# A top-p attention step with two more slots before its key transposes, and features plus bias formed one layer earlier

## The chip, the cores and the metric

The kernel runs on one core of one Trainium2 chip. Five engines work side by side, each through its own instructions in order: TensorE (PE, with its weight loads shown as PEld), VectorE (DVE), ScalarE (ACT), GpSimd (POOL) and SyncE (SP). SP, ACT and POOL also issue DMAs. The metric is the device time of one execution in microseconds (us); lower is better.

## The reference, cut to what matters

Four graph layers work on 4096 nodes with 256 features, each with the residual and a layer norm. Layer 0 is a product with the dense-stored, mostly sparse adjacency. Layer 1 runs two steps of a top-p attention beside two steps of a random walk:

```python
x = _layernorm(x + A @ (x * W))                       # layer 0
# layer 1, for n in range(2):
A  = _top_p_attention(Xa, W1, W2, W3)                 # softmax, keep the top 90 %
Xf = R @ Xf                                           # R = (S + I) / row sums
Xa = A @ Xa
Z  = Z + Xf @ U1[n].T + Xa @ U2[n].T
# after both steps:
h = X + Z
x = _layernorm(X + layernorm(h) * ln_g + ln_b)        # X: what layer 0 left
```

Layers 2 (attention over neighbours) and 3 (sum over neighbours, then a product with weights) follow. What matters here is that the end of layer 1 needs the sum X + ln_b once for each block of 128 nodes.

## The kernel before, in words

The nodes form 32 blocks of 128 (NT = 32). There are five stages in a row.

*Layer 0* (about 0 to 536 us). The first 16 blocks are dense (`dense_0`): panels of the adjacency come by SP and are multiplied on PE. While that goes on, `find_columns` looks for the nonzero columns of the other blocks and `list_columns` makes lists of them. The last 16 blocks are listed (`listed_0`): POOL gathers blocks of the adjacency (`pc`, in `pack`) and rows of features (`xg`, in `listed_steps`) by those lists. Each block has an end, `out_0`, in two halves. The first half (L475 to L481) is a layer norm on DVE and gives the features xi. The second half (L483 to L493) transposes them, projects them to keys kT and queries, writes the table `tab` (features and values for keys), and multiplies with U1 (po, L464), which gives qs and qp; ACT issues the stores. `later` (L497) starts the first half at once and runs the second half when two more ends have come. In this stage the framework's planner orders the instructions by estimated times, with program order as priority.

*Step one of layer 1* (536 to 1245 us) is written out by hand. A loop of slots (L1207) advances every active generator `narrow(I)` by one stage in each slot, the oldest first, and starts a new one every 8 slots (SLOTS), so that five or six are active. One slot of the random walk's stream `r_stream` follows (one gather each, its multiplication five slots later), and in odd slots one round of `lists`, which makes the lists of the first 16 blocks. On PE, ACT, DVE and POOL the instructions stand in exactly this order.

The stages of `narrow(I)` by slot number, counted from its start:

| slots | what is done | engine |
|---|---|---|
| 0 to 8 | logits in four chunks (multiplications 0 to 3, L1014), their exponentials (L1029), largest values (L1020) | PE, ACT, DVE |
| 9, 10 | sort of the largest (L736, L738), target (tgt, L1035), then uv and the threshold mid (L1050) | DVE, POOL |
| 11 to 20 | marks (L1058), counts (cs), ranks, offsets (pd, off, step, since), positions (pi, L1089), indices idx (L1098) | ACT, PE, DVE |
| 21 to 23 | five gathers of rows g from `tab` (L1102) | POOL |
| 24 | empty | |
| 25, 26 | key transposes pk (L1110), copy kg | PE, ACT |
| 27 to 30 | logits of the listed columns sl, reload of the features x0, exponential w, mask and its sum (L1123) | PE, SP, ACT, DVE |
| 31 to 35 | transposes pw, copy wT, weighted sum psa (L1137), new features xa, transposes ptx | PE, ACT |
| 36 to 41 | copy xT, product po (L464), copy v (L884) and features plus bias xb (L886, stored to `xbd`), z (L890), scaling and store of z, projection psq | ACT, PE, POOL, DVE, SP |

The slots of one narrow that are equal modulo 8 meet those of the others, so a cycle of 8 slots holds each stage once. The logits and the wide transposes share two banks (tag lg), the gathered rows have two sets of five tiles.

*Step two* (1245 to 2390 us) is a second top-p attention; its `out_1` (L919) loads xb back. *Layers 2 and 3* end the kernel at 2819 us. The code below is that which the change touches.

Of the kernel before, what the change touches and what calls it, by code (L numbers as in the profile page):

```python
# [11 lines left out]
F32 = mybir.dt.float32  # L12
# [6 lines left out]
P = 128  # L19
N = 4096  # L20
D = 256
# [48 lines left out]
def gnn_kernel(ctx: ExitStack, tc: tile.TileContext, x, pair, W0, W1, W2T, W3T, U1T, U2T,  # L70
               ln_g, ln_b, Hv, W3L, b3, out):
    nc = tc.nc
# [7 lines left out]
    scopes, pools = [], {}  # L80
# [28 lines left out]
    def row_bcast(v, n, name, tag=None):  # L109
        t = const.tile([P, n], F32, name=name, tag=tag or name)  # L110
        nc.gpsimd.dma_start(t, bass.AP(tensor=v.tensor, offset=v.offset, ap=[[0, P], [1, n]]))
        return t
# [4 lines left out]
    def rows(I):  # L117
        return slice(I * P, (I + 1) * P)


    XW = []
    w0b = row_bcast(W0, D, "w0b")
    for j in range(NT):
        t = big.tile([P, D + 1], F32, name=f"xw_{j}", tag=f"xa{j}", padded_shape=[P, D + 2])
        nc.scalar.dma_start(t[:, :D], x[rows(j), :])
# [14 lines left out]
    w1 = work.tile([DA, D], F32, name="w1", tag="y")  # L140
# [89 lines left out]
    def transposed(tiles, name, apart=False):  # L230

        n = 2 * len(tiles)
        pt = bank([P, 4, P], "ptx", "ms")
        for s, t in enumerate(tiles):
            for h in range(2):
                nc.tensor.transpose(pt[:, 2 * s + h, :], t[:, h * P:(h + 1) * P], ident)  # L236
        xT = work.tile([P, 4, P], F32, name=name, tag="xT")
        def turn():
            nc.scalar.copy(xT[:, :n, :], pt[:, :n, :])  # L239
        if apart:  # L240
            return turn, xT
        turn()
        return xT
# [23 lines left out]
    def layernorm(o, y, own=True):  # L267
        m, rs = norm_stats(y, own)
        nc.vector.tensor_scalar(o, y, m, rs, op0=OP.subtract, op1=OP.mult)
# [8 lines left out]
    def project(xT, n, I, more=None):  # L278

        half, b = divmod(I, NT // 2)  # L280
        r, other = (slice(h * DA, (h + 1) * DA) for h in (half, 1 - half))
        c = rows(n * (NT // 2) + b)
        ps = bank([P, 2, P], "psq", "ms")
        for h in range(2):
            nc.tensor.matmul(ps[:, 0, :], wqk[:, h, r.start:r.start + P], xT[:, h, :], start=(h == 0), stop=(h == 1))
        if more is not None:
            for h in range(2):
                nc.tensor.matmul(ps[:, 1, :DA], xT[:, h, :], wqk[:, h, :DA], start=(h == 0), stop=(h == 1))
        yield
        nc.scalar.copy(kT[r, c], ps[r, 0, :])  # L290
        q = work.tile([P, P], F32, name="q")
        nc.scalar.copy(q[other, :], ps[other, 0, :])
        (nc.sync if n else nc.scalar).dma_start(qd[n][I], q[other, :])
        if more is not None:
            nc.scalar.copy(more[:, D:], ps[:, 1, :DA])

    def run(gen):
        for _ in gen:
            pass
# [144 lines left out]
    qpd, zd, xbd = ([dram.tile([P, D], F32, name=f"{k}_{I}", tag=f"{k}{I}") for I in range(NT)] for k in ("qp", "z", "xb"))  # L444
# [7 lines left out]
    def load_u(w, pool):  # L452

        u = pools[pool].tile([P, 2, 2 * D], F32, name="u", bufs=1)
        for n in range(2):
            nc.gpsimd.dma_start(u[:, :, n * D:(n + 1) * D], w[n].rearrange("(c p) o -> p c o", p=P))
        return u
# [3 lines left out]
    def times_both(xT, u):  # L461
        po = bank([P, 2, D], "po", "ms")
        for h in range(2):
            nc.tensor.matmul(po.rearrange("p a b -> p (a b)"), xT[:, h, :], u[:, h, :], start=(h == 0), stop=(h == 1))  # L464
        return po
# [8 lines left out]
    def out_0(I, ps, sums, xin):  # L474
        nc.vector.tensor_scalar_add(rone[:, I:I + 1], sums, 1.0)  # L475
        nc.vector.reciprocal(rinv[:, I:I + 1], rone[:, I:I + 1])
        y = work.tile([P, D], F32, name="y")
        nc.vector.tensor_mul(y, ps[:, :D], w0b)
        nc.vector.tensor_add(y, y, xin)
        xi = pools["w0"].tile([P, TW], F32, name="xi", bufs=4)  # L480
        layernorm(xi[:, :D], y)  # L481
        yield
        xT = transposed([xi], "xT0")  # L483
        for _ in project(xT, 0, I, xi):
            pass
        nc.scalar.dma_start(tab[rows(I), :], xi)
        po = times_both(xT, U[0])
        qs = pools["w0"].tile([P, D], F32, name="qs")
        nc.scalar.copy(qs, po[:, 1, :])
        nc.scalar.dma_start(qtab[rows(I), :], qs)  # L490
        qp = pools["w0"].tile([P, D], F32, name="qp")
        nc.vector.scalar_tensor_tensor(qp, po[:, 0, :], rone[:, I:I + 1], qs, op0=OP.mult, op1=OP.add)
        nc.scalar.dma_start(qpd[I], qp)  # L493

    waiting = []

# [7 lines left out]
    def listed_0(I):  # L504
        pse = bank([P, 2, LC], "pse", "lg")[:, 0, :]
        ps = acc_tile("R")
        es = es_tile()
        parts = list(pack(I, es[:, 0, :], es[:, 1, :]))
        listed_matmul(ps, x, D, I, parts)
        for k in range(2):  # L510
            nc.tensor.matmul(pse[:, k:k + 1], es[:, k, :], ones, start=True, stop=True)
        nc.scalar.copy(edge[:, I:I + 1], pse[:, 0:1])
        for m, (a, b) in enumerate(pieces(I)):
            nc.scalar.dma_start(packed[I][m], parts[m][:, :b - a])
        later(out_0(I, ps, pse[:, 1:2], XW[I][:, :D]))

    def dense_0(I):
        ps = acc_tile("A")
        blocks = list(range(I * NEW, min((I + 1) * NEW, NT)))
        adj_matmul(ps, XW, I, seen, D + 1, lambda c: [find_columns(J) for J in blocks[c:c + 1]])  # L520
        later(out_0(I, ps, ps[:, D:D + 1], XW[I][:, :D]))

    late = LE
    for I in range(LE):
# [4 lines left out]
        if I >= LE // 2:  # L529
            n = (11 * (I - LE // 2 + 1)) // (LE // 2) - (late - LE)  # L530
# [13 lines left out]
    banks(lg=2)  # L544
    enter(e=2, gat=8, sp=2, w1=2)
    U[1] = load_u(U2T, "w1")
    gb, bb, hvb = row_bcast(ln_g, D, "gb"), row_bcast(ln_b, D, "bb"), row_bcast(Hv, D, "hvb")
    facts = [{k: const.tile([P, NT], F32, name=f"f{n}_{k}") for k in "sfuhxrd"} for n in range(2)]
    n_listed = const.tile([P, NT], F32, name="n_listed")
    both_sums = const.tile([P, NT, 2], F32, name="both_sums")  # L550
# [298 lines left out]
    def reload(src, I, name="xin", pool=None):  # L849
        t = (pools[pool] if pool else work).tile([P, D], F32, name=name, bufs=2)  # L850
        nc.sync.dma_start(t, src[rows(I), :D])
        return t
# [18 lines left out]
    def z_tile():  # L871
        return work.tile([P, D], F32, name="z")
# [4 lines left out]
    def out_a0(I, xa, x0, v):  # L877
        turned, xT = transposed([xa], "xT1", True)
        yield
        turned()  # L880
        yield
        po = times_both(xT, U[1])
        yield
        nc.scalar.copy(v, po[:, 1, :])  # L884
        xb = pools["w1"].tile([P, D], F32, name="xb")
        nc.gpsimd.tensor_add(xb, x0, bb)  # L886
        nc.sync.dma_start(xbd[I], xb)
        yield
        z = z_tile()
        nc.vector.tensor_add(z, po[:, 0, :], x0)  # L890
        yield
        nc.scalar.activation(z, z, AF.Copy, scale=rone[:, I:I + 1])
        nc.sync.dma_start(zd[I], z)
        yield from project(xT, 1, I)
# [101 lines left out]
    def narrow(I):  # L996
# [104 lines left out]
        for k in range(NB):  # L1101
            gather(g[k], tab, idx, slice(k, k + 1))  # L1102
            if k % 2:
                yield
        yield
        yield
        kg = sp.tile([DA, NB * P], F32, name="kg", bufs=1)
        pk = wide("pk")
        for k in range(NB):
# [7 lines left out]
        x0 = reload(tab, I, "x0r", "w1")  # L1117
# [22 lines left out]
        yield  # L1140
        V.append(v_tile(I))
        yield from out_a0(I, xa, x0, V[I])

    def wide(name):
# [45 lines left out]
    def r_stream():  # L1190
        due, t = [], 0
        for b in list(range(LE, NT)) + list(range(LE)):
            if b == 0:
                run(lists)
            for _ in r_one(b, lambda f: due.append((t + LATE, f))):
                t += 1
                while due and due[0][0] <= t:
                    due.pop(0)[1]()
                yield
        for _, f in due:  # L1200
            f()

    everything = {getattr(mybir.EngineType, k) for k in ("PE", "Activation", "DVE", "Pool")}
    with tc.manual_schedule(engines=everything):
        active, side, credit, n = [], r_stream(), 0.0, 0
        started = 0
        while active or started < NT:  # L1207
            if n % SLOTS == 0 and started < NT:
                active.append(narrow(started))
                started += 1  # L1210
            for g in list(active):
                if next(g, active) is active:
                    active.remove(g)
            credit += PACE
            while credit >= 1.0:
                next(side, None)
                credit -= 1.0
            if n % 2:
                next(lists, None)
            n += 1  # L1220
        run(side)
# [221 lines left out]
    def with_all_columns():  # L1443
        U[0], U[1] = load_u(U1T, "w0"), load_u(U2T, "w1")
        for I in range(LE, NT):
            ps = acc_tile("A")
            adj_matmul(ps, rows4(x, 1), I, width=D + 1)
            xin = reload(x, I)
            run(out_0(I, ps, ps[:, D:D + 1], xin))
# [82 lines left out]
```

## Time and profile before

| what | value |
|---|---|
| median of 3 runs | 2817.93 us (2816.73 to 2818.35) |
| the profiled execution | 2821.13 us, of which its span 2819.3 us |
| granted TensorE clock, mean | 0.908 of full speed |
| busy share of the span | PE 80%, DVE 75%, POOL 63%, PEld 56%, ACT 54% |
| DMA | 354.25 MB, mean 126 GB/s |
| gathers on POOL in step one | 160 of g, 969 ns each; 180 of xg from qtab, 979 ns each |
| xb on POOL (L886) | 32, 736 ns each, first at 623.4 us, last at 1234.3 us |
| transposes of keys (L1110) | 160, 282 ns each, first at 586.7 us, last at 1218.0 us |

The busy time of an engine says how much it has to do, and not whether the end waits for it. The waits say which instruction stood idle and what ended the idleness; the chain of waits follows the last instruction back in time. Where several engines take turns in a loop, the one that ends each wait last sets the pace.

### The profile page before, as it was taken

How to read it: one execution, taken by the hardware profiler on the slowest of the kernel's cores; microseconds unless marked ns; L12 is line 12 of the kernel's file. 1: busy time of each engine (PE TensorE's matmuls, PEld its weight loads, DVE VectorE, ACT ScalarE, POOL GpSimd, SP SyncE). 2: the span in 40 equal slices, each digit the busy share in tenths (PEclk: the TensorE clock that was granted, in tenths of full speed). 3: DMA queues.
4: the chain of work that ended last, by engine and by line, in shares of the span. 5: the costliest groups of instructions: out<-in, count | busy, mean ns of one | idle time of the engine just before them, and what ended most of it. 6: DMA issues, size and time to landing. Idle time of an engine off the chain costs nothing.

```text
span 2819.3 us, 38065 instructions
## 1 busy us (share of the span) xinstructions
PE 2256.6 (80%) x10712; PEld 1589.9 (56%) x10712; DVE 2109.3 (75%) x6442; ACT 1520.5 (54%) x2432; POOL 1781.4 (63%) x2840
## 2 busy tenths in 40 slices
PE   6778789778988888853788888888888887597997
PEld 4556576444444444531566666666656666476785
DVE  4777566688777778715688999999999997477574
ACT  0001111255566566537688888888888983464111
POOL 1002644355677667753788888888888874675774
PEclk9989898888898989875899999999999998799998
DMA  9995765444445445540212111111111112686664
GB/s 269 266 269 169 195 193 168 133 135 145 126 136 146 140 137 156 147 128 2 83 50 63 52 52 44 45 52 49 61 44 40 42 35 77 210 245 193 194 208 126
DMA packets 354060, 354.25 MB, mean 126 GB/s; under 512 B 35120, under 2 KB 307008, under 8 KB 353840
## 3 DMA queue, kind: packets, MB, share of 16 engines
q1 hardware_dynamic: 272224, 183.10, 22.3%
q0 software_dynamic: 51008, 144.85, 18.0%
q10 hardware_dynamic: 30608, 23.77, 2.6%
q8 instruction: 88, 1.44, 0.2%
q14 instruction: 132, 1.08, 0.1%
HBM read 298.69 MB, written 52.89 MB: 125 GB/s over the span
## 4 chain that ended last, share of the span: by engine, by line
PE 33%; DVE 27%; DMA 12%; POOL 11%; ACT 10%; issue 7%; ACTq 0%; DVEq 0%; POOLq 0%; SPq 0%
DMA half<-in_pair 5%; PE acc L204 4%; DVE cand L759 4%; PE po L464 4%; PE psa L228 3%; PE acc L433 3%; DVE tmp L753 3%; PE lg L1014 3%; PE acc L1363 3%; POOL xg L379 3%; DVE top L736 2%; DVE rest L738 2%; PE acc L1160 2%; DMA g<-tab,idx 2%; ACT junk L676 2%
## 5 line engine op out<-in xcount | busy, mean ns | idle before, releaser
L228 PE MATMUL psa<-v,eT 128*128 128x256 f32 x2048 | 510.7, 397 | 90.3 <-ACT eT L219 90.2
L228 PEld LDWEIGHTS psa<-v,eT 128*128 128x128 f32 x2048 | 398.2, 198 | 171.2 <-ACT eT L219 116.4
L204 PE MATMUL acc<-xw,panel 128*128 128x257 f32 x1024 | 265.5, 416 | 64.3 <-DMA panel<-in_pair 53.4
L379 POOL DMA_INDIRECT xg<-in_x,idx_x x72 | 71.5, 993 | 326.8 <-DVE idx_a L356 243.7
L204 PEld LDWEIGHTS acc<-xw,panel 128*128 128x128 f32 x1024 | 207.9, 208 | 117.8 <-issue 41.8
L676 ACT ACTIVATE junk<-e,h 128x4096 bf16<-128x4096 f32 x64 | 237.4, 3709 | 37.2 <-POOL h L656 32.0
L678 ACT ACTIVATE junk<-e,h 128x4096 bf16<-128x4096 f32 x64 | 238.3, 3723 | 0.1
L217 PE MATMUL pt<-ident,e 128*128 128x128 f32 x1024 | 157.8, 285 | 85.1 <-DVE e L805 57.9
L379 POOL DMA_INDIRECT xg<-ttab,idx_x x180 | 177.3, 985 | 67.1 <-issue 34.2
L379 POOL DMA_INDIRECT g<-tab,idx x160 | 155.0, 969 | 94.2 <-issue 50.9
L569 PE MATMUL lg<-kT,qi 64*128 64x512 f32 x512 | 157.7, 694 | 69.9 <-ACT junk L640 66.8
L379 POOL DMA_INDIRECT xg<-qtab,idx_x x180 | 176.2, 979 | 55.7 <-issue 45.6
L379 POOL DMA_INDIRECT pc<-in_pair,idx_a x180 | 174.3, 968 | 52.1 <-issue 45.8
L759 DVE MAX8 cand<-tmp 128x8 f32<-128x128 f32 x1024 | 203.3, 276 | 1.2
L217 PEld LDWEIGHTS pt<-ident,e 128*128 128x128 f32 x1024 | 130.3, 147 | 130.0 <-issue 90.7
L1020 DVE MAX8 cand<-e 128x8 f32<-128x256 f32 x512 | 179.1, 412 | 28.5 <-ACT e L1029 22.1
L1014 PE MATMUL lg<-kT,qi 64*128 64x512 f32 x512 | 168.7, 740 | 33.4 <-ACT e L1029 28.1
L219 ACT COPY eT<-pt 128x512 f32<-128x512 f32 x256 | 145.0, 592 | 85.6 <-PE pt L217 85.5
L239 ACT COPY xT<-ptx 128x256 f32<-128x256 f32 (+1 forms) x96 | 42.4, 441 | 266.2 <-PE ptx L236 129.9
L379 POOL DMA_INDIRECT xg<-x3d,idx_x x146 | 139.8, 957 | 67.2 <-issue 40.3
L637 ACT ACTIVATE e<-lg 128x1024 f32<-128x1024 f32 x128 | 131.6, 1028 | 67.6 <-PE lg L569 63.7
L1029 ACT ACTIVATE e<-lg 128x1024 f32<-128x1024 f32 x128 | 130.7, 1021 | 57.6 <-PE lg L1014 57.1
(323 smaller groups left out, 5645.8 us busy)
## 6 DMA issues: line engine op xcount, KB each, us to landing
panel<-in_pair SPq DMA_DIRECT2D x200, 256.0 KB
half<-in_pair SPq DMA_DIRECT2D x64, 512.0 KB
pc<-pk SPq DMA_DIRECT2D x55, 320.0 KB
pc<-pk SPq DMA_DIRECT2D x45, 256.0 KB
tab<-xi ACTq DMA_DIRECT2D x33, 160.0 KB
pc<-pk SPq DMA_DIRECT2D x23, 192.0 KB
x2d<-x SPq DMA_DIRECT2D x32, 129.0 KB
x<-x2d SPq DMA_DIRECT2D x32, 129.0 KB
```

The source lines that it names most:

```text
L204: nc.tensor.matmul(ps[:, :width], a[:, k, :], r, start=(j == 0), stop=stop and j == NT - 1)
L217: nc.tensor.transpose(pt[:, k, :], e[:, (g * 4 + k) * P:][:, :P], ident)
L219: nc.scalar.copy(eT[g], pt)
L228: nc.tensor.matmul(ps[:, :D], eT[g][:, k, :], rhs[j][:, :D], start=(j == 0), stop=stop and j == NT - 1)
L379: nc.gpsimd.indirect_dma_start(out=o, out_offset=None, in_=src, in_offset=bass.IndirectOffsetOnAxis(ap=idx[:, c], axis=0))
L569: nc.tensor.matmul(ps[:, h, :], qi[r, :], kT[r, (n * NC + c) * LC:][:, :LC], start=True, stop=True)
L637: nc.scalar.activation(both(e, c), ps, AF.Exp, accum_out=s8[:, c:c + 1])
L676: nc.scalar.activation(junk_tile(), e, AF.Relu, bias=h, scale=-1.0, accum_out=part)
L678: nc.scalar.activation(junk_tile(), e, AF.Sign, bias=h, scale=-1.0, accum_out=below)
L759: nc.vector.max(cand[:, c * (NS // 2) + g, :], w[:, g * SEG:(g + 1) * SEG])
L1014: nc.tensor.matmul(lgs[c][:, k, :], qi[r, :], kT[r, c * LC:(c + 1) * LC], start=True, stop=True)
L1020: nc.vector.max(cand[:, b, :], e[:, b * SEG0:(b + 1) * SEG0])
```

## The change

Four edits. The row of ln_b (bb) is loaded to all partitions at the start of the program and not at the start of layer 1. The second half of `out_0` adds it to the features on POOL and stores the sum (`xbd`) by ACT; `out_a0` in step one no longer does so (there SP stored it). Behind the gathers, `narrow` yields four times where it yielded twice, so that every stage from the key transposes on stands two slots later, in slots 27 to 43. The rounds of `lists` begin in slot 3 and not in slot 1.

```diff
-    w0b = row_bcast(W0, D, "w0b")
+    w0b, bb = row_bcast(W0, D, "w0b"), row_bcast(ln_b, D, "bb")
@@ out_0
         nc.scalar.dma_start(qpd[I], qp)
+        xb = pools["w0"].tile([P, D], F32, name="xb")
+        nc.gpsimd.tensor_add(xb, xi[:, :D], bb)
+        nc.scalar.dma_start(xbd[I], xb)
@@ start of layer 1
-    gb, bb, hvb = row_bcast(ln_g, D, "gb"), row_bcast(ln_b, D, "bb"), row_bcast(Hv, D, "hvb")
+    gb, hvb = row_bcast(ln_g, D, "gb"), row_bcast(Hv, D, "hvb")
@@ out_a0
         nc.scalar.copy(v, po[:, 1, :])
-        xb = pools["w1"].tile([P, D], F32, name="xb")
-        nc.gpsimd.tensor_add(xb, x0, bb)
-        nc.sync.dma_start(xbd[I], xb)
         yield
@@ narrow
             if k % 2:
                 yield
-        yield
-        yield
+        for _ in range(4):
+            yield
         kg = sp.tile([DA, NB * P], F32, name="kg", bufs=1)
@@ the loop of slots
-            if n % 2:
+            if n % 2 and n > 2:
                 next(lists, None)
```

## The prediction

> **What bounds the kernel now.** I read the page first: the chain that ended last is spread over PE 33%, DVE 27%, DMA 12% and POOL 11%, so no engine bounds the whole, and the change must be judged in its two stages. Next came the busy times by stage (columns: stretch, its length, busy PE, PEld, DVE, ACT, POOL, then PEclk, DMA share, GB/s): the part of layer 0 in which listed tiles run, and step one.
>
> ```profile
> 259.00:536.00 277.00, 224.56 (x992) 170.21 (x991) 164.77 (x491) 35.34 (x136) 141.40 (x146) 0.89 0.60 172
> 536.00:1245.00 709.00, 591.94 (x3307) 335.20 (x3307) 529.46 (x1851) 404.24 (x720) 479.76 (x593) 0.89 0.50 143
> ```
>
> In step one PE is busy for 83% and POOL for 68%, but two gathers start 1.25 us apart though each is busy 0.95, so POOL is nearly full too. Then the waits of 560 to 1240 us (total us, times, longest):
>
> ```profile
> PE pk L1110 <- DMA g<-tab,idx: 54.5, 36, 4.4
> ...
> PEld lg L1014 <- ACT e L1029: 34.4, 21, 3.3
> ...
> ACT marks L1058 <- DVE mid L1050: 31.0, 24, 3.5
> ...
> DVE z L890 <- ACT v L884: 21.3, 13, 7.0
> ...
> DVE uv L1045 <- POOL tgt L1035: 13.0, 11, 3.0
> ```
>
> PE waits 54.5 us for gathered keys, but it also waits for exponentials, which come late because ACT waits for the threshold (mid) from DVE. The chain of waits shows both in one cycle of eight slots:
>
> ```profile
> 909.95 2.00 ACT marks L1058
> 911.95 1.01 ACT e L1029 x2
> 912.96 0.04 issue
> 913.00 1.13 PE lg L1014 x4
> ...
> 922.48 4.25 DMA g<-tab,idx
> 926.73 0.04 issue
> 926.77 0.30 PE pk L1110
> ```
>
> So there are two loops of about equal length. Loop A: indices (DVE) end at 913.59, five gathers leave POOL until 923.42, the last key transpose starts at 926.77, and the next indices follow it on PE and DVE. Loop B: logits multiplication 3, its exponential, the largest values, the sort, mid, marks, exponential 1, multiplication 2, and on to multiplication 3. By the timeline, multiplication 2 of narrow 8 starts at 714.56 and that of narrow 31 at 1169.17: 23 cycles of 19.77 us. Eight cycles in which loop B alone rules (it starts 0.14 us after exponential 1 at both ends) take 18.37, 20.68, 19.87, 18.72, 18.71, 19.78, 18.14, 19.55: 19.23 on average. Removing the wait for the gathers is therefore not worth 54.5 us.
>
> Last, the POOL rows around an addition of features and bias, and a stretch of layer 0's chain:
>
> ```profile
> 917.82 0.73 POOL L886 TENSOR_TENSOR xb<-x0r,bb 128x256 f32<-128x256 f32 x1
> ...
> 918.71 0.97 POOL L379 DMA_INDIRECT g<-tab,idx  x1 [0.16 <-issue]
> ```
> ```profile
> 415.27 5.03 DMA pc<-in_pair,idx_a
> 420.43 0.69 DVE pr L400
> ```
>
> One addition holds POOL for 0.89 us, in the midst of the five gathers. In layer 0, POOL's gathers of pair blocks and their landing are themselves on the chain.
>
> **What the Trainium skill says.** "TensorE: Matmul & The Clock Gate", Part 1: an idle window of about 3.4 us halves PE's clock. The trace agrees: in 987.4 to 1001.0, right after waits for gathers, PEclk is 0.50; po (four passes) takes 3.31 us at 895.56 against 1.72 elsewhere. Same page, "Architectural detail": ACT, DVE and GpSimd are strict FIFO. Here the store of a packed block held ACT until 420.48 and the copy xT behind it until 421.82. "Trainium Kernel Development and Optimization", Key Constraints: transfers issued from SP, ACT and POOL share the same 16 DMA engines, so the store's move from SP to ACT moves no bytes elsewhere; only its time changes (no row before tests it). "GPSIMD Engine Reference", Engine selection: a two-input elementwise operation there is about twice as slow as on VectorE; the trace has 736 ns (L886) against 414 ns (L890, same shape).
>
> **The change, part by part.** Sums are made against the profiled execution: 2821.13 us (span 2819.3), 3.2 us above the median of 2817.93.
>
> *Two slots, gain on the gathers.* Between the slot of the last gather and that of the transposes lie four slots (some 10 us) where two lay. New loop A: indices, 0.76 us to the first gather, seven gathers of 1.25 less a gap (8.45), 3 us to land, then pk and pi (0.8) and the next indices (2.1): 15 us, below loop B, so this wait should nearly vanish. Its worth is how much later than exponential 1 multiplication 2 now starts, beyond 0.14: in narrows 9, 10, 12 to 15, 19 to 22 and 29 it is 0.58, 4.02, 0.08, 1.63, 1.23, 0.90, 0.16, 1.97, 1.89, 2.02 and 1.89, in sum 16.4 us. The averages above give (19.77 − 19.23) × 23 = 12.4. I take 16.4, bounds 12 and 30 (halved clock behind a wait lengthens the multiplications after it).
>
> *Two slots, cost on the order.* Everything from the transposes to the projection shifts by two places in the cycle. (1) z (L890, 0.41 us, 0.45 with its gap) stood in DVE's order before the largest values of chunk 3, in the shadow of ACT's exponential; now it stands between them and the sort, inside loop B: 0.45 × 28 cycles = +12.6. It also waits for v and so for po, now one slot after multiplication 3: at full clock po ends as DVE comes free, so +0; at half clock up to 1.7 us more. Bounds 0 (PE later anyway) and +25. (2) The mask and its reciprocal (L1123, L1125: 1.1 us) leave a gap of DVE for the place just before chunk 3; where multiplication 3 starts under 4.5 us after multiplication 2 (six of 23 cycles) this costs about 0.6: +3.6. (3) PE's work between the same multiplications is equal (po 1.72 leaves, ptx 0.43 and sl 1.3 come in). Logits banks still alternate; multiplication 3 now needs exponential 2's bank, free 3.9 us after multiplication 2 against a measured minimum of 3.75: nothing. Gather tiles g have two sets; the weighted sum that frees them moves to two slots ahead of the gathers that reuse them: no wait. The tail's two empty slots cost nothing, as the last narrow waits for its gathers there anyway.
>
> *Addition off step one.* POOL loses 32 × 0.89 = 28 us, SP 32 stores (and the 171 us that SP spent waiting for POOL). POOL's target (tgt) stands behind the gathers and held DVE's uv for 13.0 us, inside loop B; without 0.89 us ahead of it and with z in front of uv that goes: −13.0, bounds 0 and −13. The last narrow's gathers end 0.9 earlier.
>
> *Addition in layer 0.* 32 POOL additions and 32 ACT issues (0.33 us as L493), 4.2 MB. POOL is idle until 259.15, so early ones are free. Later, by program order, an addition stands between a listed tile's feature gathers and the next tile's block gathers. The chain passes that junction some eight times (near 271, 284, 313, 329, 364, 411, 477, 498): 8 × 0.89 = +7.1, bounds 0 (the planner puts it into a stall; POOL stands 63.8 us waiting for PE's L433) and 2 × 7.1. Behind it wait the block gathers, DVE's pr and PE. ACT's new store waits for POOL; behind it are xT, kT and qs copies, for which PE waits. I take 0, upper bound ten times 1 us. Bytes: 4.2 MB at 172 GB/s is 24 us of transfer beside 60% busy queues, hidden; I take +0.5. At the end one more store (0.33) precedes the landing that POOL waits for: +0.4. The bias row's load moves to the start, where POOL is idle: 0.
>
> *Lists.* One of 32 list rounds (1.4 us of DVE) moves from slot 1, where DVE waited, to the end of the rounds: +0.7. The last lump runs in slot 65 instead of 63, before slot 72 needs it.
>
> Sum: −16.4 + 12.6 + 3.6 − 13.0 − 0.9 + 7.1 + 0.5 + 0.4 + 0.7 = −5.4 us: 2815.7 against the profiled execution, 2812.5 against the median. About 0.2% (5.6 us) can be told from no change.
>
> **Rivals.**
> 1. *Order loses in step one* (slower). z and the mask lengthen loop B in every cycle, PE's idle time gathers in one wait ahead of multiplication 2, the clock halves there each time, and po in the slot behind multiplication 3 holds v, z and the sort: +25 for z, only −12 for the gathers, −6 for tgt, +3.6, layer 0 +9: +20, 2838. For it: clocks of 0.50 in 891.8 to 898.6 and 1014.7 to 1021.5, where no gather was late. Against: DVE has only 75% to do. It decides once z starts over 1 us after chunk 3's largest values.
> 2. *Clock recovers.* The halved stretches behind late gathers (13.6 us at 748 and 987, 10.3 at 1123) go too: −30 − 13 − 1 + 16 + 8 = −20, 2798. Against: PE still waits for exponential 1.
> 3. *Hidden anyway*: the gathers' wait is replaced in full by loop B and z eats tgt's gain: −12 − 6 + 13 + 4 + 8 = +7, 2825.
>
> **How the numbers follow.** Forecast (2803 to 2821) 0.43, rival 1 0.18, rival 2 0.19, rival 3 0.20. Faster by over 0.2%: 0.24 of the forecast's share and rival 2: 0.43. Within: 0.16 and 0.04 of rival 3: 0.20. Slower: 0.03, 0.16 and 0.18: 0.37. The range, 2793 to 2840, spans both signs; the forecast's own is 2803 to 2821.
>
> **What would show it.** Right: the wait of pk for g under 10 us in step one, uv for tgt under 3, cycles near 19.3. Wrong: z waiting over 20 us in front of the sort; pk still waiting (then POOL, not the slots, is late); layer 0 longer than 536 us by over 12 or with ACT waiting for POOL; step one ending at the same distance from its start.

## The result, and the profile after

The changed kernel takes 2860.41 us (median of 4 runs, 2855.28 to 2865.41) where the kernel before takes 2817.33 us beside it (4 runs, 2810.70 to 2818.35). The ratio is 1.0158, with a 95% interval of 1.0134 to 1.0182: slower by some 43 us. Of the experiments below, e1 to e4 ran where the kernel before takes 2822 us; beside all later ones it takes 3088 to 3129 us, through waits that are described with them, so every run is read as a ratio to the kernel before beside it.

The profiled executions have spans of 2819.3 and 2863.6 us. The difference of 44.3 us falls so: layer 0 up to the first logits 536.6 to 541.0 us (+4.4), step one 708.3 to 740.9 us (+32.6), everything after it 1574.4 to 1581.7 us (+7.3). The last part runs code that the change leaves alone; over the four experiments beside it that part takes 1573 to 1578 us, so about half of the 7 us lies within the scatter between executions, and the rest is not explained here. What has to be explained is step one.

The busy times of step one after (columns as in the view of before: stretch, length, busy PE, PEld, DVE, ACT, POOL, then PEclk, DMA share, GB/s):

```profile
541.00:1282.00 741.00, 618.51 (x3307) 353.81 (x3308) 527.91 (x1854) 400.41 (x720) 456.77 (x560) 0.83 0.46 131
```

PE has the same 3307 matmuls as before but is busy for 618.5 us instead of 591.9, at a granted clock of 0.83 instead of 0.89; its idle time goes from 117.1 to 122.5 us. DVE, ACT and POOL have no more to do than before. So PE ran slower by 27 us in all. How much of that lies where the end waits for it has to be read from the loop.

The waits of step one after (560 to 1280 us; total us, times, longest):

```profile
ACT marks L1058 <- DVE mid L1050: 92.7, 28, 7.1
PEld lg L1014 <- ACT e L1029: 84.9, 39, 4.2
...
DVE z L890 <- ACT v L887: 13.4, 11, 2.5
...
PE pk L1110 <- DMA g<-tab,idx: 3.4, 2, 3.1
```

The wait of the key transposes for the gathers has gone from 54.5 to 3.4 us, and no line of DVE's uv waiting for POOL's target is left among the answers. In their place ACT waits 92.7 us for mid (31.0 before), and PE's weight loads wait 84.9 us for the exponential ahead of a multiplication (34.4 before). What waits now does not wait for memory or POOL: the loop through DVE, ACT and PE, loop B of the prediction, now binds in nearly every cycle.

How that loop got longer can be laid out from the timeline. The table follows one cycle from multiplication 2 of one narrow to that of the next, in us, as means over the 23 cycles from narrow 8 to narrow 31; e1, e2 and e4 are explained below. The pieces are the time differences between instructions of the PE, ACT and DVE timelines.

| piece of loop B | before | after | e1 | e2 | e4 |
|---|---|---|---|---|---|
| start of multiplication 2 to start of 3 | 5.34 | 5.62 | 5.72 | 5.06 | 7.31 |
| multiplication 3 | 1.13 | 1.66 | 1.66 | 1.13 | 2.05 |
| its end to chunk 3's largest values | 1.56 | 2.03 | 1.95 | 1.47 | 1.55 |
| largest values, (z), sort, mid | 7.86 | 7.99 | 7.99 | 7.63 | 7.28 |
| mid to the end of exponential 1 | 3.03 | 3.09 | 3.09 | 3.02 | 3.07 |
| exponential 1 to multiplication 2 | 0.85 | 0.14 | 0.14 | 0.65 | 0.44 |
| cycle | 19.77 | 20.54 | 20.55 | 18.95 | 21.71 |
| multiplication 3 wholly or partly at half clock, of 27 cycles from narrow 4 | 0 | 16 | 16 | 0 | 26 |
| PE idle just ahead of multiplication 2, in one piece | 0.67 | 2.40 | 2.44 | 0.74 | 0.42 |

The row of the cycle says +17.7 us for the 23 cycles. The four cycles from narrow 4 to narrow 8 bring +18.4 more (96.3 us before, 114.7 after), and the start and the end of the step give back 3.6. Of the 18.4 us, 9.7 lie in the cycle from narrow 7 to narrow 8, in which the last lump of the lists now stands behind the largest values (slot 65) and not ahead of them (slot 63).

In those early cycles it can be seen what stands in the way. PE in the kernel before, behind multiplication 3 at 647.71 (columns of the timeline: start, length, engine, line, operation, and in brackets the idle time before it and what ended it):

```profile
647.71 1.13 PE L1014 MATMUL lg<-kT,qi 64*128 64x512 f32 x4
648.77 0.70 PE L1160 MATMUL acc<-xg,pc 128*128 128x256 f32 x2
649.31 0.71 PE L1130 MATMUL pw<-ident,w 128*128 128x128 f32 x5
649.85 0.60 PE L1160 MATMUL acc<-xg,pc 128*128 128x256 f32 x2
```

and DVE there:

```profile
650.49 0.42 DVE L856 TENSOR_TENSOR y<-acc,xin 128x256 f32<-128x256 f32 x1 [1.99 <-PE acc L1160]
...
652.22 1.40 DVE L1020 MAX8 cand<-e 128x8 f32<-128x256 f32 x4
```

The same place in the kernel after, PE:

```profile
650.74 2.08 PE L1014 MATMUL lg<-kT,qi 64*128 64x512 f32 x4
652.75 1.22 PE L1160 MATMUL acc<-xg,pc 128*128 128x256 f32 x2
653.76 2.49 PE L464 MATMUL po<-u,xT 128*128 128x512 f32 x4
656.08 0.59 PE L1160 MATMUL acc<-xg,pc 128*128 128x256 f32 x2
```

and DVE:

```profile
656.71 0.42 DVE L859 TENSOR_TENSOR y<-acc,xin 128x256 f32<-128x256 f32 x1 [5.19 <-PE pd L1076]
...
658.45 1.40 DVE L1020 MAX8 cand<-e 128x8 f32<-128x256 f32 x4
659.76 0.41 DVE L890 TENSOR_TENSOR z<-po,x0r 128x256 f32<-128x256 f32 x1
```

y is the random walk's sum. Its instruction has its fixed place in DVE's order, here ahead of chunk 3's largest values, and it needs the last of the walk's multiplications (acc) on PE. Behind multiplication 3 PE used to do the transposes pw (0.71 us) before that multiplication; now it does po, which is four passes, and all of it at half clock: 2.08, 1.22 and 2.49 us. So y starts 5.97 us after multiplication 3 instead of 2.78, and the largest values, whose exponential ended at 653.9, come after it, 7.71 us behind multiplication 3 instead of 4.51. (The trace names pd as what ended y's wait; y reads acc, whose last multiplication ended at 656.7 too.) z, the addition that the forecast priced, is one line of 0.41 us in that stretch.

In the 23 cycles of the table y stands last ahead of chunk 3's largest values in six, the same six in both kernels (narrows 8, 15, 17, 22, 25 and 29). In these, the time from the end of exponential 3 to the largest values is 15.4 us in sum after and 6.1 before. That is 9.4 of the 10.3 us by which this time grew over all 23 cycles.

The clock can be read from the traces too. In those of before, after and e1 to e4 the granted clock changes only on a grid of 3.413 us (within 5 ns over the whole execution). In step one of the six, 139 of the 146 windows of this grid that were at full clock with PE busy for less than half of the window were followed by half clock, and 36 of the 739 busier ones. So what counts is mostly how idle one window is, and not the length of one idle piece: in narrow 15 of the changed kernel 2.12 us of idle time lie in one window and the clock halves; in narrow 26 the edge of a window cuts 2.79 us into 1.41 and 1.38, and it doesn't.

Step one has no more stretches at half clock after (26) than before (27), but they are longer: 9.5 us on average instead of 6.0, in sum 247 us instead of 162. Within a window's length of the start of multiplication 2 the clock falls in 9 of the 27 cycles before and in 17 after. Before, it is back at full ahead of multiplication 3 in all 9; after, in 1 of 17. Here are windows of the grid (columns as above, the third number from the end is PEclk) in narrow 17 of the kernel before, with multiplication 2 at 892.33, po at 895.35 and multiplication 3 at 900.09:

```profile
891.80:895.22 3.42, 2.89 (x6) 1.30 (x7) 2.99 (x7) 3.42 (x6) 2.73 (x3) 0.50 0.57 169
895.22:898.63 3.41, 3.41 (x5) 1.20 (x5) 2.78 (x9) 0.82 (x2) 2.70 (x4) 0.50 0.40 124
898.63:902.04 3.41, 3.41 (x45) 2.31 (x44) 1.03 (x4) 1.14 (x2) 2.79 (x3) 1.00 0.51 138
```

and in narrow 16 of the kernel after, with multiplication 2 at 899.71, multiplication 3 at 906.77 and po at 909.78:

```profile
897.32:900.73 3.41, 1.02 (x4) 0.30 (x4) 2.65 (x11) 3.39 (x6) 2.39 (x3) 1.00 0.36 111
900.73:904.14 3.41, 3.41 (x8) 1.79 (x7) 2.61 (x6) 3.02 (x4) 2.50 (x4) 0.50 0.36 101
904.14:907.56 3.42, 3.42 (x39) 2.45 (x39) 2.46 (x9) 0.70 (x1) 2.81 (x3) 0.50 0.51 135
907.56:910.97 3.41, 3.41 (x8) 1.50 (x5) 0.93 (x3) 1.11 (x2) 2.50 (x3) 0.50 0.42 111
```

Before, po stood between the two multiplications, and in eight of the nine cycles the last window at half clock holds a part of it. After, ptx and sl stand there in its place, and in the other 16 cycles the clock comes back only 3.5 to 5.8 us behind the start of multiplication 3. That po brought the clock back is a reading of these traces; no run tests it alone.

### The profile page after: what moved, and what is told of

Its sections match the earlier page's. It is cut to its first block, busy times and chain, and to the rows that moved or that the text cites. A ratio compares the mean times of both kernels' runs of the same rounds, so it can differ in the third digit from the quotient of the medians.

```text
span 2863.6 us, 38050 instructions
## 1 busy us (share of the span) xinstructions
PE 2284.7 (80%) x10712; PEld 1611.6 (56%) x10712; DVE 2109.0 (74%) x6442; ACT 1514.9 (53%) x2432; POOL 1782.0 (62%) x2840
## 4 chain that ended last, share of the span: by engine, by line
PE 18%; DVE 17%; POOL 8%; ACT 8%; issue 4%; DMA 2%; SPq 0%; DVEq 0%; POOLq 0%; ACTq 0%
DVE cand L762 4%; PE psa L228 4%; PE acc L433 3%; DVE tmp L756 3%; PE acc L1363 3%; ACT junk L679 2%; PE pz L869 2%; PE lg L572 2%; POOL xg L379 2%; DVE top L739 2%; DVE rest L741 1%; PE acc L204 1%; ACT junk L681 1%; DVE e L808 1%; ACT e L640 1%
## 5 line engine op out<-in xcount | busy, mean ns | idle before, releaser
L1014 PE MATMUL lg<-kT,qi 64*128 64x512 f32 x512 | 173.9, 761 | 79.4 <-ACT e L1029 73.9
L572 PE MATMUL lg<-kT,qi 64*128 64x512 f32 x512 | 158.3, 691 | 70.5 <-ACT junk L643 66.4
L495 POOL TENSOR_TENSOR xb<-xi,bb 128x256 f32<-128x256 f32 x32 | 23.9, 748 | 262.5 <-DVE xi L269 189.4
L1058 ACT ACTIVATE marks<-e,mid 128x2048 bf16<-128x2048 f32 x64 | 128.3, 2004 | 100.7 <-DVE mid L1050 92.7
L1029 ACT ACTIVATE e<-lg 128x1024 f32<-128x1024 f32 x128 | 130.7, 1021 | 78.6 <-PE lg L1014 78.1
```

What stands on the lines that cost most here:

```text
L572: nc.tensor.matmul(ps[:, h, :], qi[r, :], kT[r, (n * NC + c) * LC:][:, :LC], start=True, stop=True)
L1014: nc.tensor.matmul(lgs[c][:, k, :], qi[r, :], kT[r, c * LC:(c + 1) * LC], start=True, stop=True)
L1029: nc.scalar.activation(both(e, c), lgs.pop(c), AF.Exp, accum_out=sq[:, c:c + 1])
```

## The experiments

**Which part of the change: slots or addition (e1, e2).** e1 is the kernel before with the slots alone; the lists begin a round later as in the change.

```diff
-        yield
-        yield
+        for _ in range(4):
+            yield
...
-            if n % 2:
+            if n % 2 and n > 2:
```

> The kernel before with the two more slots alone (and the list rounds begun one later); the addition stays in step one. Theory A (order: behind logits multiplication 3 now stand po on PE and the mask, y and z on DVE, all inside loop B, and PE idles in one piece ahead of multiplication 2): most of the loss is here, 2840 to 2860 us, with the first logits at 536.6 us as before and cycles of 20.3 us or more. Theory B (the addition's new place in layer 0 carries the loss): at most 2825 us.

Measured: 2855.16 us, ratio 1.0111 (1.0083 to 1.0139). Theory B falls. The cycles are within 0.02 us those of the changed kernel (20.55 and 20.54 us, 16 of 27 halved), though POOL still does the additions there. One number was not expected: the first logits came at 530.3 us, 6.3 us earlier than before with the same program up to there apart from the lists, so 4.4 us more in layer 0 is not a difference that one execution can tell.

e2 is the kernel after with the slots taken back.

```diff
-        for _ in range(4):
-            yield
+        yield
+        yield
...
-            if n % 2 and n > 2:
+            if n % 2:
```

> The kernel after with the two slots taken back; the addition stays at the ends of layer 0. Theory A: layer 0 some 4 us longer, step one 5 to 13 us shorter since POOL has 28 us less to do between gathers: 2805 to 2818 us. Theory B: 2830 us or more.

Measured: 2816.59 us, ratio 0.9983 (0.9969 to 0.9996). The addition's move alone gains a little, about 5 us, the only version here that is faster than before. Waits of its step one (560 to 1230 us):

```profile
PE pk L1110 <- DMA g<-tab,idx: 47.5, 35, 2.6
...
DVE uv L1045 <- POOL tgt L1035: 6.5, 7, 1.1
```

uv's wait for POOL's target has halved (13.0 us before) and that for the gathers is 7 us shorter. In its profiled execution, which with a span of 2803.7 us is one of its fastest, the cycle is 0.81 us shorter. With the two slots this gain is gone: e1 and the changed kernel have the same cycle with and without the additions on POOL, because neither the gathers nor the target bind there any more (in e1 uv waits 1.9 us).

**Which place in the order (e3, e4).** Here z alone, and then po with v and z, go two slots later; the last round of the lists moves to a slot where its two banks are free.

```diff
# e3
         nc.scalar.copy(v, po[:, 1, :])
-        yield
+        for _ in range(3):
+            yield
         z = z_tile()
# e4
         turned()
-        yield
+        for _ in range(3):
+            yield
         po = times_both(xT, U[1])
# both
-            if n % 2 and n > 2:
+            if n % 2 and 2 < n < 65:
...
+                if n == 67 and g is oldest:
+                    next(lists, None)
```

> The kernel after with z (and the projection behind it) two slots later, out of the sort's slot; po and the copy v stay one slot behind multiplication 3. If z's own time and its wait for v are the loss in step one, some 0.9 us in each of 28 cycles comes back: 2835 us or less. If po behind multiplication 3 is the loss (DVE's y of the other stream waits for PE behind it, and the clock is halved there), z alone brings little: 2848 to 2862 us.

> The kernel after with po, v, z and the projection two slots later: po then fills PE while loop B is in the sort, the stretch in which PE waits for exponential 1 anyway. Theory A: multiplication 3 is followed at once by the short multiplications, y no longer waits behind po, the wait ahead of multiplication 2 falls below 2 us and the clock stays up: 2805 to 2828 us, cycles below 19.8 us. Rival (the loss comes from the transposes, the mask or the gathers' new place, none of which moves here): still 2845 us or more.

Measured: e3 2911.9 us, ratio 1.0311 (1.0287 to 1.0336); e4 2891.66 us, 1.0251 (1.0226 to 1.0275). e3 fell outside what either theory gave; e4 came out in the rival's range, 2845 us or more. But in both the order of the change is mixed with something that neither expectation had: ptx, po and psq share one bank, and with psq two slots later the next ptx has to wait for psq's copies. PE in one cycle of e4, where lines stand one further down than in the kernel after:

```profile
906.41 1.13 PE L1015 MATMUL lg<-kT,qi 64*128 64x512 f32 x4 [0.75 <-ACT e L1030]
907.47 0.70 PE L1161 MATMUL acc<-xg,pc 128*128 128x256 f32 x2
910.09 0.44 PE L236 MATMUL ptx<-ident,xa 128*128 128x128 f32 x2 [1.92 <-ACT q L292]
```

ptx stands behind multiplication 2, so the whole of PE waits there, 1.9 us in this cycle and 62.5 us in sum (61.9 in e3). What the edit was meant to show is in the table nevertheless: with po and z out of the way the stretch from multiplication 3 to mid shrank (1.55 and 7.28 us, below the kernel before), and PE's idle time ahead of multiplication 2 fell to 0.42 us, as theory A said. But multiplication 3 ran at half clock in 26 of 27 cycles. Part of the idle time had only moved to the other side of multiplication 2, as in these lines; but in the cycles of narrows 25 and 29 no idle piece from 5 us ahead of multiplication 2 up to multiplication 3 is longer than 0.75 us, and multiplication 3 takes 2.08 us there too. That less idle time ahead of multiplication 2 is enough to keep the clock up, as theory A had it, is refuted. Of the 36 times that the clock falls in step one of e4, 24 follow a window with PE busy for under half, as elsewhere; the falls of narrows 25 and 29 follow windows with PE busy for 78%.

**Later runs, among waits of another kind.** e5 moves ptx with po, v, z and psq, so that the bank is asked for in the old order (the lists as in e3 and e4):

```diff
         xa = new_xa(pools["w1"].tile([P, D], F32, name="xa"), psa, rk)
-        yield
+        for _ in range(3):
+            yield
```

e6 gives PE more to do ahead of multiplication 2, e7 leaves z's addition out, e8 has one slot instead of two:

```diff
# e6
-        for k in range(NB):
+        for k in 3 * list(range(NB)):
             nc.tensor.transpose(pk[:DA, k * P:(k + 1) * P], g[k][:, D:], ident)
# e7
         z = z_tile()
-        nc.vector.tensor_add(z, po[:, 0, :], x0)
         yield
-        nc.scalar.activation(z, z, AF.Copy, scale=rone[:, I:I + 1])
+        nc.scalar.activation(z, x0, AF.Copy, scale=rone[:, I:I + 1])
# e8
-        for _ in range(4):
+        for _ in range(3):
             yield
...
-            if n % 2 and n > 2:
+            if n == 66 or n % 2 and 2 < n < 65:
```

> The kernel after with ptx, its copy, po, v, z and the projection all two slots later, so that the one bank that ptx, po and psq share is asked for in the order of before (moving po alone made ptx wait 1.9 us for psq's copies just behind multiplication 2). Theory A (po and y behind multiplication 3, z ahead of the sort, and PE idle in one piece): no wait of ptx, multiplication 2 to 3 about 5.3 us again, largest values to mid below 6.2 us, cycles below 19.6 us: 2800 to 2830 us. Rival (PE work in any slot behind a wait halves the clock, wherever po stands): multiplication 3 still takes 2.08 us in most cycles, 2845 us or more.

> The kernel after with each key transpose issued three times into the same place: 1.4 us more PE work per tile, one slot before multiplication 2, where PE waits 2.7 us for exponential 1. If PE's idle piece ahead of multiplication 2 is what halves the clock behind it (multiplication 3 takes 2.08 us in 16 of 28 cycles), the clock stays up, multiplication 3 takes 1.13 us in nearly all cycles and 0.5 to 1.5 us a cycle come back although work was added: 2820 to 2848 us. If the clock is only a companion, nothing comes back: 2857 to 2890 us.

> The kernel after without DVE's addition z: ACT scales x0 alone, so z is the features without po's half; all else stays. What z costs in its new place, with its wait for v: theory A as forecast, 0.45 us in each of 28 cycles and the wait of 13.4 us in sum: 2832 to 2848 us. If po behind multiplication 3 (through y and the clock) carries the loss and z only fills time: 2850 to 2862 us.

> The kernel after with one more slot than before instead of two: z stands in the slot of chunk 3's largest values, ahead of them, and po in the slot of multiplication 3, ahead of it. The gathers' wait should fall by half or more (one slot is 2.4 us). If the loss is the place in the cycle and not the longer way as such, this differs from both: 2810 to 2840 us. If each slot costs alike, half the loss of the slots: 2830 to 2842 us.

From here on the kernel before takes 9 to 11% longer too, so none of these times could be held against its expectation, and the kernel after was run again beside three of them:

> The changed kernel once more, as the measure for the three runs beside it: on the first chip its ratio to the kernel before was 1.0158, with cycles of 20.5 us and multiplication 3 halved in 16 of 28. On a chip where the exponential of chunk 3 waits some 7 us in every cycle for something that the trace calls remote, all ratios are of that wait too.

> The kernel after with ptx, its copy, po, v, z and the projection two slots later (as e5, where the waits called remote hid the answer). Theory A (po, y and z inside loop B behind multiplication 3): ratio to before 0.990 to 1.004, cycles below 19.6 us where no remote wait stands. Rival (any PE work moved so halves the clock): 1.010 or more.

> The kernel after with each key transpose issued three times: 1.4 us more PE work per tile in the place where PE waits for exponential 1. If PE's idle piece halves the clock and that is much of the loss: below the ratio of after by 0.004 or more, multiplication 3 at 1.13 us in nearly all cycles. If the clock is only a companion: at or above the ratio of after.

> The kernel after without DVE's addition z (ACT scales x0 alone; po's half is left out of z). If z between the largest values and the sort is the loss: below the ratio of after by 0.006 or more (0.45 us and half a us of wait in 28 cycles). If po behind multiplication 3 carries it through y, mask and clock: within 0.004 of the ratio of after.

The same waits stood in all runs that followed, among them g1 and g2, which had the chip of e1 to e4; so they don't belong to one chip.

> Each key transpose three times, as f2, in the hope of a chip without the waits called remote. In cycles without such waits: if PE's idle piece ahead of multiplication 2 halves the clock and that is the loss, multiplication 3 takes 1.13 us in nearly all cycles and the ratio to before falls from 1.0158 (after) to 1.011 or less; if the clock is only a companion, or the work costs as much as the clock gives, 1.015 or more.

> ptx to projection two slots later, as f1. Without remote waits theory A gives 0.990 to 1.004 and cycles below 19.6 us, because po, y and z leave the stretch from multiplication 3 to mid; if the clock is halved all the same, as in f1 where it brought nothing (1.0273 beside 1.0269), 1.012 or more.

> ptx to projection two slots later, as f1 and g2, which both fell among the remote waits. Without them theory A gives a ratio of 0.990 to 1.004 and cycles below 19.6 us; the rival (the clock is halved all the same) 1.012 or more. Among remote waits again: 1.024 to 1.030, as before.

> One more slot than before instead of two, as e8 (1.0095 among remote waits, where after has 1.0269). Without remote waits: z ahead of chunk 3's largest values and po ahead of multiplication 3. If the places behind multiplication 3 carry the loss, 0.996 to 1.006; if each slot costs alike, 1.007 to 1.011.

> ptx to projection two slots later, as f1, g2 and h1, which all fell among the remote waits. Without them theory A gives a ratio of 0.990 to 1.004 and cycles below 19.6 us; the rival (the clock is halved all the same) 1.012 or more. Among remote waits again: 1.024 to 1.030.

| kernel | ratios to before (each with its 95% interval) |
|---|---|
| after (f0) | 1.0269 (1.0234 to 1.0305) |
| ptx to psq two slots later (e5, f1, g2, h1, k1) | 1.0235 (1.0196 to 1.0274), 1.0273 (1.0236 to 1.0309), 1.0265 (1.0232 to 1.0298), 1.0259 (1.0229 to 1.0290), 1.0296 (1.0236 to 1.0356) |
| keys thrice (e6, f2, g1) | 1.0271 (1.0225 to 1.0318), 1.0318 (1.0290 to 1.0346), 1.0315 (1.0283 to 1.0346) |
| z's addition left out (e7, f3) | 1.0195 (1.0157 to 1.0234), 1.0234 (1.0207 to 1.0262) |
| one slot more than before (e8, h2) | 1.0095 (1.0066 to 1.0124), 1.0094 (1.0062 to 1.0125) |

A last run gave the trace of the kernel before among these waits.

> The kernel before, for a trace among the remote waits. If the waits are the chip's and not the change's, exponential 3 waits 5 to 7 us in most cycles here too, and the cycles are some 24 us where after has 25.5; if the change draws them, before has few of them and its 280 us more lie elsewhere.

It took 3088.38 us, with cycles of 22.2 us. ACT in one cycle of f0:

```profile
903.64 1.02 ACT L1029 ACTIVATE e<-lg 128x1024 f32<-128x1024 f32 x1 [8.45 <-remote]
```

Exponential 3 waits 8.45 us for multiplication 3, which PE's records end at 896.98, and DVE's has waits as long for cs, recorded as ended at 894.98. By the semaphore events of the trace PE's signals for cs, multiplication 3 and po came at 903.56, 903.62 and 903.68, in one burst, 8.6, 6.6 and 3.6 us after the recorded ends. On average over narrows 8 to 30 the time from multiplication 3's recorded end to its exponential is 2.9 us in the kernel before (k2; neither the 5 to 7 us nor the few waits of its expectation), 5.3 and 5.6 with one slot (e8, h2), 6.2 in the kernel after (f0), 6.3 to 7.4 in the five runs with ptx to psq later, and 0.05 to 0.07 us in the traces of before, after, e1 and e2 above. Every kernel traced there has these waits, and every one with more slots has more of them. Why PE's signals come late, and why the order of the slots changes how often, no run here shows.

What follows from the five kinds of run, with that reserve. Moving ptx to psq out of loop B brings nothing measurable beside f0 (in f1 the stretch from the largest values to mid falls from 7.69 to 7.35 us, but the wait behind multiplication 3 grows from 6.2 to 6.5). More PE work ahead of multiplication 2 makes multiplication 3 run at half clock in 3 instead of 7 of 27 cycles (f2 against f0), and yet the kernel is slower by 0.5% (its six runs, 3190 to 3200 us, lie above the four of f0 beside them, 3177 to 3181): multiplication 2 itself now starts 0.97 us after exponential 1 instead of 0.24. Leaving z's addition out shortens the stretch of the sort by 0.36 us a cycle, 8 us over 23 cycles; the whole is 0.35% lower (its six runs, 3163 to 3172 us, lie below the four of f0). One slot costs a third of what two cost, so among these waits the cost is not the same for each slot; whether it is so without them, no run shows.

## Why the prediction was wrong, step by step

*Right: the gathers' wait.* 16.4 us were forecast for multiplication 2 starting later than exponential 1 allows. The table has 0.85 and 0.14 us, times 23 cycles 16.3 us. The mark set for pk, under 10 us, was met with 3.4, and e1 shows that the slots do it without the addition's move (2.4 us). The mark for the cycle, near 19.3 us, was missed with 20.54.

*Wrong: the term "PE's work between the same multiplications is equal", priced at nothing.* This is the step that failed. It counted what PE does between two multiplications and found the sums alike; it left out the order in which it is done and the clock at which. Measured over the 23 cycles: multiplication 2 to 3 +0.28, multiplication 3 +0.54, its end to the largest values +0.47 us, together +1.29 us a cycle or 30 us: 6 and 12 us in the first two pieces, 9.4 us in the six cycles with y. In the four early cycles, 18.4 us more, of which 10 lie between the end of exponential 3 and mid and 6.6 from the start of multiplication 2 to the end of multiplication 3. po, moved from in front of multiplication 3 to behind it, stands there ahead of the walk's multiplication, and y, which waits for that on DVE ahead of the largest values, was named nowhere in the prediction. That the loss belongs to the slots, with the lists' start that moves with them, is shown by e1, where both stand without the addition's move, and by e2, where both are absent. The lists' start alone was not run. That y waits behind po, and that the clock falls more often at multiplication 2 and comes back later, is read from the traces: e3 and e4, which were to test it, brought a wait of their own, and e5, f1 and f2 ran where other waits hid what the order was worth. So which edit loses is shown; how the loss is shared between po's place and the clock is not.

*Nearly right in sum, and each smaller: z (+12.6) and the target (−13.0).* Together they were −0.4 us; from the largest values to mid the table has +0.13 us a cycle, +2.9 us. z waited 13.4 us for v, below the 20 that were to be the sign of failure: a late z was not what lost. f3 puts z's own part at 0.36 us a cycle, where 0.45 was forecast. The target's 13.0 us were counted beside the gathers' 16.4, as if both could be had. e2 has its part of the one without the slots, the changed kernel has the other; e1 against the changed kernel shows that with the slots the addition's move adds nothing to the cycle.

*Right in kind, and smaller: the mask (+3.6).* In four of the 23 cycles (narrows 10, 12, 19 and 24) the mask, its reciprocal and the ranks behind them ran on into the place of the largest values, which cost 2.3 us in sum; before, z had cost 1.5 us there in four cycles. Multiplication 3 started under 4.5 us after multiplication 2 in seven cycles of the kernel before, and not in six as was counted.

*Not told apart: layer 0 (+7.1, +0.5, +0.4).* Layer 0 is 4.4 us longer in the changed kernel and 4.0 in e2, less than forecast, beside a scatter of 6 us that e1 shows. The four traces with the addition there have their first logits at 540.7 to 542.9 us, the two without at 530.3 and 536.7: some cost is likely, and its size is open. The wait of ACT's new store for POOL, taken as nothing, did come: in 30 of the 32 blocks the store starts at the end of POOL's addition, up to 7.9 us after ACT's instruction before it, and the copy kT behind it stood for 12.1 us in sum in five blocks. That was among the prediction's signs of being wrong; what it cost the whole is not shown.

*The rivals.* Rival 1 had the direction and most of the mechanism: PE's idle time gathers in one wait ahead of multiplication 2 (0.67 to 2.40 us a cycle, while PE's idle pieces of over 0.25 us only went from 2.61 to 2.66 us a cycle in sum), the clock halves there in 17 cycles instead of 9, and po behind multiplication 3 holds what follows. It was priced at +20 and its deciding point was put at z. The point was met in some cycles (z started 1.26 us after the largest values at 912.70), but the loss lay at y and the clock, and was twice as large. Rival 2, the clock recovering, was the opposite of what came: 0.89 to 0.83. The range of 2793 to 2840 ended at rival 1's price and so missed 2860.

The Trainium skill's statement in "TensorE: Matmul & The Clock Gate", Part 1, that an idle window of about 3.4 us halves PE's clock, was cited in the prediction and used there only for bounds and rivals. Its length is that of the grid in these traces. But the window need not be idle as a whole: PE busy for under half of it was enough in 139 of 146 cases, 2.12 us of idle time in one window among them. At 987.4 us of the kernel before, where the prediction saw agreement, the idle time came in pieces of 0.98, 1.06 and 2.23 us, and the window ahead had PE busy for 0.60 of its 3.41 us. Where the page and the traces differ, the measurement decides.

## What to carry to other kernels

When a stage moves in an order written by hand, list for each engine what now stands directly behind the multiplication that the loop waits for, and then everything on other engines that waits for PE behind it, from other streams too: equal sums between two points say nothing about who is served first. Two waits that end at the same instruction are worth their union: removing both pays once. And PE's clock is a term of its own in such a sum: the same matmuls, with 5 us more idle time, were busy for 27 us longer in another order, so an order whose clock can't be foretold needs a range to the slow side as wide as that. To foretell it, look at how idle PE is in each stretch of 3.4 us, and at what it does between there and the multiplication that the loop waits for.

## What the runs showed of the hardware that was not expected

PE's clock goes by windows of 3.413 us in these traces, and a window at full clock with PE busy for under half of it was followed by half clock in 139 of 146 cases. That is not the whole rule: 36 of 739 busier windows were followed by half clock too, 12 of them in e4 and 9 in e3. Nor does a busy window by itself bring the clock back: in step one of the changed kernel 32 windows at half clock had PE busy for over 92% and were followed by half clock again. What else enters is open.

In the later runs PE's signals reached ACT and DVE in bursts up to 8.6 us after the recorded end of the matmul, in every kernel traced and on the same chip that had shown none of it before. The kernel before took 9 to 11% longer there, and the changed one 2.7% instead of 1.6% longer than it. How much of the 9 to 11% is these waits was not measured: of the 267 us in k2's trace, step one has 108.
